# Score matmuls of a graph attention layer: two 64x128 array tiles or four 64x64 array tiles

## The chip, the cores and the metric

The kernel runs on one core of one Trainium2 chip. The metric is the device time of one execution in microseconds, the median of several runs. All data and all matmuls are in float32.

## The reference

For 128 graphs of 128 nodes with 768 features, a layer norm and a ReLU are followed by attention with 12 heads of 64 features. The adjacency matrix of each graph is both mask and bias of the scores. The result is added to the input.

```python
h = jnp.maximum(_layernorm(x, axis=-1), 0.0)
q = _split_heads(h @ Wq + bq)          # 12 heads of 64
k = _split_heads(h @ Wk + bk)
v = _split_heads(h @ Wv + bv)
scores = jnp.einsum('bhqd,bhkd->bhqk', q, k) / jnp.sqrt(HD)
scores = scores + beta * adj[:, None]
scores = jnp.where(adj[:, None] > 0, scores, -9e15)
probs = jax.nn.softmax(scores, axis=-1)
out = jnp.einsum('bhqk,bhkd->bhqd', probs, v)
x = x + out                            # heads side by side again
```

## The kernel before

Graphs are taken in 32 groups of four. The projections (Q, K and V) are computed by a scheme of 15 block products per slice of the output columns; each product is four matmuls of a full 128x128 weight tile with 256 moving columns:

```python
for i in range(2):
    for c in range(2):
        ...
        nc.tensor.matmul(p[:, i, :], lhs, rhs, start=(first and i == 0 and c == 0), stop=(c == 1),
                         skip_group_check=True)
```

The products are evicted and summed by ScalarE and VectorE (tiles pa, pb, pc and pd are the four banks that they go through). A tile `qk` holds, for two heads and two graphs, the queries in `t[:, 0]` and the keys in `t[:, 1]`, the 64 features of the first head on partitions 0 to 63 and those of the second on 64 to 127.

The scores of two heads (`oc`) and four graphs are eight matmuls. The keys are the stationary operand (64 rows, 128 columns), the queries the moving one (128 columns). Each head goes to its own bank of PSUM. The scores lie with the keys on the partitions:

```python
def scores(G, oc):
    u, j = oc // 3, oc % 3
    ...
    ps = [psum.tile([P, GRP, N], F32, tag="at", name=f"sc_{G}_{oc}_{i}") for i in range(2)]
    for g in range(GRP):
        t = qk[G, f"qk{u}", g // 2, j]
        at = slice((g % 2) * N, (g % 2 + 1) * N)
        for i in range(2):
            r = slice(i * HD, (i + 1) * HD)
            nc.tensor.matmul(ps[i][:, g, :], t[r, 1, at], t[r, 0, at], start=True, stop=True)
    for i in range(2):
        e = es[G, oc, i] = work.tile([P, GRP, N], F32, tag="e", name=f"e_{G}_{oc}_{i}")
        nc.vector.scalar_tensor_tensor(e, ps[i], SCORE_CAP * ISCALE, biasT[G], op0=ALU.min, op1=ALU.add)
        nc.scalar.activation(e, e, AF.Exp, scale=1.0 / ISCALE)
```

VectorE evicts them with the bias and the mask added, ScalarE takes the exponential in place. The product with V follows four block products later. Here the exponentials are the stationary operand, 64 queries at a time, so that the two halves go to the two halves of the array's columns; the moving operand is V with a column of ones beside it, 65 columns, which gives the sum of each softmax too:

```python
def attend(G, oc):
    o = work.tile([P, 2, 4, HD], F32, tag="o", name=f"o_{G}_{oc}", bufs=2)
    for r in range(2):
        pa = psum.tile([P, 4, VE], F32, tag="at", name=f"av_{G}_{oc}_{r}")
        for g in range(2):
            for i in range(2):
                h = 2 * oc + i
                for q in range(0, P, HD):
                    nc.tensor.matmul(pa[q:q + HD, 2 * g + i, :], es[G, oc, i][:, 2 * r + g, q:q + HD],
                                     vt[G, "v", r, h // 4][:, 4 * g + h % 4, :], start=True, stop=True)
        weigh(G, oc, r, pa, o[:, r])
    ...
```

`scores_half` and `attend_half` do the same for two graphs at a time and are used for three of the six head pairs of the last group. Scores and V products stand between the block products; of three score blocks in a slice the second and the third follow directly on a V block:

```python
def attention(G, u):
    todo = {}
    for i in range(3):
        todo.setdefault(1 + 4 * i, []).append(lambda oc=3 * u + i: scores(G, oc))
        todo.setdefault(5 + 4 * i, []).insert(0, lambda oc=3 * u + i: attend(G, oc))
    return todo
```

Of the kernel before, what the change touches and what calls it, by code (L numbers as in the profile page):

```python
# [106 lines left out]
def direct(ctx, tc, x, adj, wq, bq, wk, bk, wv, bv, beta, out, bad):  # L107
# [10 lines left out]
    nc = tc.nc  # L118
    B, N, D = x.shape
    HD = D // HEADS  # L120
# [224 lines left out]
    def scores(G, oc):  # L345
        u, j = oc // 3, oc % 3
        t = xo[G, oc] = work.tile([P, GRP, P], F32, tag="xo", name=f"xo_{G}_{oc}", bufs=3)
        nc.sync.dma_start(t, x[G * GRP:(G + 1) * GRP, :, oc * P:(oc + 1) * P].rearrange("g n d -> n g d"))
# [3 lines that stand above are left out]
            at = slice((g % 2) * N, (g % 2 + 1) * N)  # L352
            for i in range(2):
                r = slice(i * HD, (i + 1) * HD)
                nc.tensor.matmul(ps[i][:, g, :], t[r, 1, at], t[r, 0, at], start=True, stop=True)  # L355
        for i in range(2):
            e = es[G, oc, i] = work.tile([P, GRP, N], F32, tag="e", name=f"e_{G}_{oc}_{i}")
            nc.vector.scalar_tensor_tensor(e, ps[i], SCORE_CAP * ISCALE, biasT[G], op0=ALU.min, op1=ALU.add)  # L358
            nc.scalar.activation(e, e, AF.Exp, scale=1.0 / ISCALE)  # L359
# [27 lines left out]
    def scores_half(G, oc, r):  # L387

        u, j = oc // 3, oc % 3
        g0 = G * GRP + 2 * r  # L390
        t = xo[G, oc, r] = work.tile([P, 2, P], F32, tag="xo", name=f"xo_{G}_{oc}_{r}", bufs=3)
        nc.sync.dma_start(t, x[g0:g0 + 2, :, oc * P:(oc + 1) * P].rearrange("g n d -> n g d"))
        ps = [psum.tile([P, 2, N], F32, tag="at", name=f"sc_{G}_{oc}_{r}_{i}") for i in range(2)]
        t = qk[G, f"qk{u}", r, j]
        for g in range(2):
            for i in range(2):
                h = slice(i * HD, (i + 1) * HD)
                nc.tensor.matmul(ps[i][:, g, :], t[h, 1, g * N:(g + 1) * N], t[h, 0, g * N:(g + 1) * N],
                                 start=True, stop=True)
        e = es[G, oc, r] = work.tile([P, 2, 2, N], F32, tag="e", name=f"e_{G}_{oc}_{r}")  # L400
        for i in range(2):
            nc.vector.scalar_tensor_tensor(e[:, i], ps[i], SCORE_CAP * ISCALE, biasT[G][:, 2 * r:2 * r + 2, :],
                                           op0=ALU.min, op1=ALU.add)
            nc.scalar.activation(e[:, i], e[:, i], AF.Exp, scale=1.0 / ISCALE)
# [16 lines left out]
# [7 lines that stand above are left out]
# [72 lines left out]
    for G in range(NG):  # L500
# [27 lines left out]
        if G + 1 < NG:  # L528
            got = []
            at = 1 if G else 6  # L530
# [34 lines left out]
        for at, f, *args in (  # L565
            (0, scores, 0), (3, attend, 0), (3, scores, 1), (6, attend, 1), (6, scores, 2), (9, attend, 2),
            (9, scores_half, 5, 0), (10, scores_half, 4, 0), (11, attend_half, 5, 0), (12, scores_half, 3, 0),
            (12, attend_half, 4, 0), (13, scores_half, 3, 1), (13, attend_half, 3, 0), (14, scores_half, 5, 1),
            (14, attend_half, 3, 1), (14, scores_half, 4, 1), (14, attend_half, 5, 1), (14, attend_half, 4, 1),
        ):  # L570
            then(at, lambda f=f, args=args: f(G, *args))
# [143 lines left out]
```

## Time and profile before

| what | value |
|---|---|
| time, median of 3 runs | 3005.92 us (3005.69 to 3007.42) |
| span of the profiled run | 3006.0 us |
| granted TensorE clock | 0.998 |
| records of matmuls, and of weight loads | 20918 each |
| of these, scores on line 355 | 3024 |
| of these, V products on line 380 | 6048 |
| VectorE evictions of scores, 128x512 | 378, mean 684 ns |

In the lines of the profile, PE is TensorE's matmuls, PEld its weight loads, DVE VectorE, ACT ScalarE, POOL GpSimd. A name with an L is a line of the kernel. A pair such as 64*128 gives the rows and columns of the array that a matmul uses, and 64x128 behind it the partitions and columns of the operand read. Every float32 matmul of the program shows as two records of a weight load and two of a matmul. The recorded ends of matmuls are modelled and overlap, so the busy time of PE is not its streaming; the chain of work that ended last and the starts of single records say more.

### The profile page before, as it was taken

The numbers are of one execution on the slowest core, as the hardware profiler recorded it, in microseconds if no ns is written. First come the engines' busy times: TensorE is split into PE (matmuls) and PEld (weight loads), VectorE is DVE, ScalarE is ACT, GpSimd is POOL, SyncE is SP. The second block draws the span as 40 slices with busy tenths as digits, with TensorE's granted clock in tenths as the row PEclk, the third lists the DMA queues.
The fourth block names the chain that finished last, engine by engine and source line by source line (L and its number), as shares of the span: only waits on it lengthen the run. The fifth ranks groups of instructions, "written<-read, shape, count | busy, mean of one in ns | idle before, by whom it ended". The sixth has DMA issues, their size and how long they took to land.

```text
span 3006.0 us, 52526 instructions
## 1 busy us (share of the span) xinstructions
PE 2985.7 (99%) x20918; PEld 2579.4 (86%) x20918; DVE 1996.6 (66%) x5155; ACT 797.3 (27%) x1703; POOL 359.7 (12%) x307
## 2 busy tenths in 40 slices
PE   8999999999999999999999999999999999999998
PEld 7888888888888888888888888888888888888887
DVE  7867567676676665676656767567676676665665
ACT  2332322322223222222222232322322222222221
POOL 1111111111110111111111111111111110111110
PEclk9999999999999999999999999999999999999999
DMA  5212122121121211221212212122121122111211
GB/s 160 71 50 57 42 58 67 50 60 43 50 68 55 55 47 45 68 60 50 60 42 58 66 52 57 41 55 68 50 60 43 50 67 57 53 51 39 64 36 40
DMA packets 358505, 170.33 MB, mean 57 GB/s; under 512 B 84464, under 2 KB 358128, under 8 KB 358256
## 3 DMA queue, kind: packets, MB, share of 16 engines
q1 hardware_dynamic: 355392, 166.14, 20.1%
q8 instruction: 166, 2.72, 0.4%
q10 hardware_dynamic: 2864, 0.79, 0.1%
q14 instruction: 83, 0.68, 0.1%
HBM read 116.53 MB, written 50.33 MB: 56 GB/s over the span
## 4 chain that ended last, share of the span: by engine, by line
PE 98%; DVE 1%; DMA 0%; ACT 0%; issue 0%; SPq 0%; ACTq 0%; DVEq 0%
PE pc_qk L316 18%; PE pb_qk L316 15%; PE pa_qk L316 15%; PE pc_v L316 9%; PE pb_v L316 7%; PE pa_v L316 7%; PE pd_qk L316 7%; PE av L380 7%; PE sc L355 7%; PE pd_v L316 4%; PE plain L445 1%; DMA x<-in_x_dram 0%; ACT x L259 0%; DVE A L266 0%; DVE qk_T L199 0%; PE pm L228 0%
## 5 line engine op out<-in xcount | busy, mean ns | idle before, releaser
L384 POOL TENSOR_TENSOR xo<-xo,o 128x512 f32<-128x512 f32 x189 | 242.1, 1281 | 2330.5 <-DVE seen L370 2300.9
L359 ACT ACTIVATE e<-e 128x512 f32<-128x512 f32 x378 | 232.8, 630 | 691.4 <-DVE e L358 690.7
L259 ACT ACTIVATE x<-x,shift,rstd 128x192 f32<-128x192 f32 x512 | 228.0, 533 | 569.4 <-POOL shift L250 569.4
L316 PE MATMUL pb_qk<-S,qk_T 128*128 128x256 f32 x1512 | 370.3, 388 | 0.0
L337 ACT ACTIVATE qk<-pc_qk,bqk 128x256 f32<-128x256 f32 x378 | 160.4, 466 | 701.5 <-PE pc_qk L316 701.5
L358 DVE SCALAR_TENSOR_TENSOR e<-sc,biasT 128x512 f32<-128x512 f32 x378 | 242.8, 684 | 110.1 <-PE sc L355 110.1
L316 PEld LDWEIGHTS pb_qk<-S,qk_T 128*128 128x128 f32 x1512 | 277.3, 190 | 44.1
L341 DVE TENSOR_TENSOR qk<-qk,pb_qk 128x512 f32<-128x512 f32 x252 | 171.9, 682 | 146.5 <-PE pb_qk L316 125.7
L316 PE MATMUL pc_qk<-S,qk_B 128*128 128x256 f32 x1008 | 245.1, 386 | 2.3 <-ACT qk L337 2.3
L380 PEld LDWEIGHTS av<-v,e 128*64 128x64 f32 x6048 | 192.6, 138 | 62.9 <-issue 43.0
L316 PE MATMUL pa_qk<-S,qk_T 128*128 128x256 f32 x1008 | 244.8, 386 | 0.0
L316 PE MATMUL pc_qk<-S,qk_T 128*128 128x256 f32 x1008 | 238.2, 379 | 0.0
L266 DVE STREAM_TRANSPOSE A<-x 128x256 f32<-128x256 f32 x384 | 217.5, 611 | 7.4 <-ACT x L259 7.3
L355 PE MATMUL sc<-qk 64*128 64x128 f32 x3024 | 219.9, 285 | 0.0
L380 PE MATMUL av<-v,e 128*64 128x65 f32 x6048 | 218.8, 225 | 0.0
L316 PEld LDWEIGHTS pc_qk<-S,qk_B 128*128 128x128 f32 x1008 | 186.7, 190 | 32.7 <-ACT qk L337 2.7
L316 PEld LDWEIGHTS pc_qk<-S,qk_T 128*128 128x128 f32 x1008 | 191.8, 190 | 25.8
L316 PEld LDWEIGHTS pa_qk<-S,qk_T 128*128 128x128 f32 x1008 | 186.5, 190 | 30.2
L355 PEld LDWEIGHTS sc<-qk 64*128 64x128 f32 x3024 | 183.8, 188 | 29.6 <-issue 20.9
L316 PE MATMUL pb_v<-v_T,S 128*128 128x256 f32 x768 | 184.0, 383 | 0.0
L341 DVE TENSOR_TENSOR qk<-qk,pd_qk 128x512 f32<-128x512 f32 x126 | 86.7, 688 | 139.0 <-PE pd_qk L316 139.0
L272 DVE TENSOR_TENSOR S<-A,A 128x512 f32<-128x512 f32 x224 | 164.2, 747 | 1.0
(117 smaller groups left out, 4520.9 us busy)
## 6 DMA issues: line engine op xcount, KB each, us to landing
x<-in_x_dram SPq DMA_DIRECT2D x504, 96.0 KB, 2.4
xo<-in_x_dram SPq DMA_DIRECT2D x189, 256.0 KB, 2.9
out_dram<-xo SPq DMA_DIRECT2D x189, 256.0 KB, 2.2
adj<-in_adj_dram SPq DMA_DIRECT2D x128, 64.0 KB, 2.3
qk_T<-in_L_gnn_Wq_dram SPq DMA_DIRECT2D x10, 128.0 KB, 3.1
qk_T<-in_L_gnn_Wk_dram SPq DMA_DIRECT2D x10, 128.0 KB, 3.2
v_T<-in_L_gnn_Wv_dram SPq DMA_DIRECT2D x5, 256.0 KB, 6.0
qk_B<-in_L_gnn_Wq_dram SPq DMA_DIRECT2D x8, 128.0 KB, 3.3
```

Source lines behind the costliest of these rows:

```text
L259: nc.scalar.activation(t, t, AF.Relu, bias=shift[G, n], scale=rstd[G, n])
L266: last = nc.vector.transpose(t[:, :, g * N:(g + 1) * N].rearrange("p c (b i) -> p c b i", i=SQ), src)
L272: nc.vector.tensor_tensor(t, A[G, a], A[G, b], ALU.add if sign > 0 else ALU.subtract)
L316: nc.tensor.matmul(p[:, i, :], lhs, rhs, start=(first and i == 0 and c == 0), stop=(c == 1), skip_group_check=True)
L337: nc.scalar.activation(t[:, i, :], p[:, i, :], AF.Identity, bias=bqk[:, i, oc:oc + 1], scale=float(sign))
L341: added[G] = nc.vector.tensor_tensor(t, t, p, ALU.add if sign > 0 else ALU.subtract)
L355: nc.tensor.matmul(ps[i][:, g, :], t[r, 1, at], t[r, 0, at], start=True, stop=True)
L358: nc.vector.scalar_tensor_tensor(e, ps[i], SCORE_CAP * ISCALE, biasT[G], op0=ALU.min, op1=ALU.add)
L359: nc.scalar.activation(e, e, AF.Exp, scale=1.0 / ISCALE)
L380: nc.tensor.matmul(pa[q:q + HD, 2 * g + i, :], es[G, oc, i][:, 2 * r + g, q:q + HD], vt[G, "v", r, h // 4][:, 4 * g + h % 4, :], start=Tru ...
L384: nc.gpsimd.tensor_add(t, t, o.rearrange("p a (b j) d -> p (a b) (j d)", j=2))
L445: nc.tensor.matmul(p[:, i, :], b[:, c, i * P:(i + 1) * P], a[:, c, :], start=(k == 0 and i == 0 and c == 0), stop=(c == 1), skip_group_che ...
```

## The change

Each score matmul is split into two, of 64 keys each. The stationary operand is then 64 rows by 64 columns, and the two halves of the keys go to the two halves of the partitions of the same bank. With two heads this addresses four tiles of the array, 64x64 each, where before it was two, 64x128 each. The moving operand, the 128 queries, is unchanged and is streamed once for each half of the keys. The aim is to keep all four tiles at work, beside V matmuls which already use two column tiles.

```diff
             for i in range(2):
                 r = slice(i * HD, (i + 1) * HD)
-                nc.tensor.matmul(ps[i][:, g, :], t[r, 1, at], t[r, 0, at], start=True, stop=True)
+                for k in range(0, N, HD):
+                    nc.tensor.matmul(ps[i][k:k + HD, g, :], t[r, 1, at][:, k:k + HD], t[r, 0, at],
+                                     start=True, stop=True)
@@
                 h = slice(i * HD, (i + 1) * HD)
-                nc.tensor.matmul(ps[i][:, g, :], t[h, 1, g * N:(g + 1) * N], t[h, 0, g * N:(g + 1) * N],
-                                 start=True, stop=True)
+                for k in range(0, N, HD):
+                    nc.tensor.matmul(ps[i][k:k + HD, g, :], t[h, 1, g * N + k:g * N + k + HD],
+                                     t[h, 0, g * N:(g + 1) * N], start=True, stop=True)
```

The second part of the diff is in `scores_half`.

## The prediction

> **What bounds the kernel now.** I read the page's first two parts, then the chain that ended last, then the waits, and last the matmuls of one short stretch.
>
> ```profile
> PE 2985.7 (99%) x20918; PEld 2579.4 (86%) x20918; DVE 1996.6 (66%) x5155; ACT 797.3 (27%) x1703; POOL 359.7 (12%) x307
> ...
> PE 98%; DVE 1%; DMA 0%; ACT 0%; issue 0%; SPq 0%; ACTq 0%; DVEq 0%
> PE pc_qk L316 18%; PE pb_qk L316 15%; PE pa_qk L316 15%; PE pc_v L316 9%; PE pb_v L316 7%; PE pa_v L316 7%; PE pd_qk L316 7%; PE av L380 7%; PE sc L355 7%; PE pd_v L316 4%; PE plain L445 1%; DMA x<-in_x_dram 0%; ACT x L259 0%; DVE A L266 0%; DVE qk_T L199 0%; PE pm L228 0%
> ```
>
> TensorE is 98% of the chain, so the time is what the matmul stream takes from end to end. The score matmuls (tile sc) are 7% of it, some 210 us of 3006; the V matmuls (av) are another 7%. In the list of waits TensorE waits for VectorE, ScalarE and the transfers about 15 us in all, nearly all at the start and the end, and VectorE is busy 66%: no other engine is close. The granted clock is 0.998.
>
> A piece of the chain from the middle of the run, columns start us, length us, what:
>
> ```profile
> 1017.65 1.73 PE pa_qk L316 x8
> 1019.38 1.08 PE av L380 x32
> 1020.46 1.09 PE sc L355 x16
> 1021.55 1.93 PE pc_qk L316 x8
> 1023.48 1.73 PE pb_qk L316 x8
> ```
>
> Eight records of a product take 1.73 us, 216 ns each, but 1.93 us behind scores: the way out of a score block costs 0.20 us. With the 1.09 us of the block itself, **a score block costs the stream 1.29 us**. There are 189 such blocks (3024 records of 16 each) and six half-sized ones in the last group. Each fp32 matmul of the program is two records, a pass each: 1536 score matmuls, 3072 records.
>
> The same stretch, asked for sc and for av (minimum/median/maximum ns):
>
> ```profile
> L355 PEld LDWEIGHTS sc<-qk x16: 183/188/189, 1020.4 to 1021.2; 64*128 64x128 f32 x16
> L355 PE MATMUL sc<-qk x16: 272/272/373, 1020.4 to 1021.3; 64*128 64x128 f32 x16
> ...
> L380 PEld LDWEIGHTS av<-v,e x32: 133/138/140, 1019.3 to 1020.2; 128*64 128x64 f32 x32
> L380 PE MATMUL av<-v,e x32: 219/222/271, 1019.3 to 1020.2; 128*64 128x65 f32 x32
> ```
>
> The first matmuls of a score block last 373 ns and the others 272: the first ones stand 101 ns waiting for their own weights, 128 columns. The first V matmuls wait only 271 - 222 = 49 ns, for 64 columns. Record by record, the score matmuls start in pairs, 6 ns apart, one in each half of the array's rows, and the pairs follow each other every 112 ns: eight rounds. The V matmuls also start in pairs, one in each half of the columns, every 59 ns. Ahead of both blocks, and behind the scores, lies a pause: from where the last matmul should have ended streaming to the next weight load some 95 ns pass (last product start 1018.998[...], first V load 1019.306). So the 1.29 us are about 95 pause + 101 weights + 8 x 112 rounds + 95 pause + 105 weights of the product behind (its first matmul takes 484 where the others take 379), which is 1292 ns.
>
> **What the Trainium skill says.** "TensorEngine Tiling (Array Packing)", Key Properties: changing the tiling mode, unlike changing the tile, drains the engine, and tiles can load and multiply side by side. The trace agrees with both: the 95 ns pause stands at each switch, and the pairs overlap. "TensorE: Matmul & The Clock Gate", LDWEIGHTS: a load costs by its columns, not its rows; the 101 ns for 128 columns and 49 ns for 64 agree. The same page, Part 3, gives about 4 ns per tile of stagger and speedups for 16 small tiles; the trace shows 6 ns, with two tiles only. "PSUM — Partial Sum Buffer", bank collisions: column tiles may write one bank together, row tiles may not. Here the row halves write different banks (ps[0] and ps[1]) before and after. No run so far shows four tiles together.
>
> **The change part by part.** It replaces each 64x128 score matmul by two of 64x64. Score matmuls go from 1536 to 3072, records from 3072 to 6144, and loads likewise, each of 64 columns in place of 128. The moving data stays 128 queries, so a matmul streams as long as before (112 ns a round). A full block becomes 32 records; with four tiles at work at once that is again 32 / 4 = **eight rounds of 112 ns**, no fewer. The array was already fully covered by two 64x128 tiles; a finer cut gives no throughput. What changes is at the edges:
>
> - The exposed first weight load falls from 101 to 49 ns: -52 ns a block, on the path.
> - The third and fourth tile start behind the second by 6 ns each: +12 ns a block, on the path.
> - The pauses at the switches stay: the mode ahead is still a different one (whole array, or 128 rows by 64 columns), and so is the product's behind. 0.
> - The product's first weights behind the block have 128 columns as before: 0.
>
> Sum: -40 ns a block, times 189, is -7.6 us; the six half blocks add -0.2. That makes **3005.9 - 7.8 = 2998 us**.
>
> Comparing the order of the built instructions: on TensorE the sequence of products, scores and V blocks is the same; ScalarE and GpSimd have no change of order; VectorE has its 5232 instructions in a somewhat different order (for instance in the middle groups a sum of activations S<-A,A moves ahead of a score eviction). As the evicted scores are needed four products (7 us) later, and one such sum takes 0.75 us, I count this as 0, with a few us of doubt at the start, where the waits of TensorE lie.
>
> **The rivals.**
>
> 1. Four tiles do not run at once. If only two of the four advance together, a block takes 16 rounds: + 8 x 112 = 0.90 us a block, x 189 = +169 us, 3175 us. For it: this kernel has never shown four tiles, and each matmul's two passes stand together in the program, so the engine must look past six records to reach the fourth tile. Against it: two row tiles and two column tiles both overlap fully now, from their first round on, with the same kind of double passes. I give it one chance in fifteen.
>
> 2. The supply of instructions becomes the bound. A score block would use up 32 loads and 32 matmuls in 0.90 us, a pair each 28 ns. The V block already keeps a pair each 59 / 2 = 29 ns for 32 pairs. But 126 score blocks follow directly on V blocks (as in the stretch above), where today 48 pairs pass in 1.08 + 1.09 = 2.17 us, 45 ns a pair, and afterwards 64 must pass in about the same time, 33 ns a pair. Nothing in the profile shows a run of 64 pairs at that pace. If 45 ns were the sustained limit, 64 x 45 = 2.88 us, +0.71 x 126 = +90 us, 3095 us. One chance in fifteen, with smaller versions of it possible.
>
> 3. The switch between two column-tiled modes (128x64 to 64x64) costs no drain. Then 126 blocks save the pause of 95 ns and hide the remaining 49 ns of weights besides: -0.144 x 126 = -18 us, 2980 us. For it: the columns are cut alike in both. Against it: the skill speaks of the mode as a whole, and every change of shape in this trace has its pause. One chance in eight.
>
> 4. VectorE becomes the bound through its new order. It idles a third of the time, so at most a few us.
>
> **Range and chances.** The centre is the sum, 2998. The lower end leaves room for the cheap switch, 2976. The upper end takes a mild shortage of instructions (some 0.2 us in each of the 126 blocks, +25 us) or a few more ns a round, 3032; the two full bad cases lie above it. Faster by over 2% would need 60 us out of blocks whose streaming cannot shrink: 0.32 us of each 1.29, more than all that the edges offer short of losing both pauses; 1%. Slower by over 2% are rivals 1 and 2 in full: 12%.
>
> **What would show it.** In the profile after: score matmuls about 6050 on their main line, still near 272 ns, and their loads near 138 in place of 188; a block's share of the chain 1.05 us in place of 1.09 (the first step right), with the product behind it still 1.93 (the pauses stayed). Records in fours, 6 ns apart, every 112 ns show the eight rounds; fours that fall into two pairs 112 ns apart are rival 1; rounds that begin at 112 ns and stretch later in a block, most of all behind V blocks, are rival 2. A score block behind V well below 1 us with no pause ahead is rival 3. The prediction is wrong if a round costs more than 112 ns with four tiles for a reason that the pairs do not show, such as loads or moving reads of the four tiles getting in each other's way: each 10 ns a round is 8 x 189 x 10 ns = 15 us.

## The result and the profile after

The changed kernel takes 2995.95 us (median of 6 runs), the kernel before in the same sessions 3006.78 us: a ratio of 0.9964, 95% interval 0.9951 to 0.9977. That is 10.8 us less, well outside the spread of either kernel (2.4 us); the prediction had 7.8 us less, 2998 us, and a range of 2976 to 3032.

The page after, its first part and the chain that ended last:

```profile
PE 2974.5 (99%) x23990; PEld 2555.1 (85%) x23990; DVE 1996.6 (67%) x5155; ACT 797.8 (27%) x1703; POOL 373.7 (12%) x307
...
PE 98%; DVE 1%; DMA 0%; ACT 0%; issue 0%; SPq 0%; ACTq 0%; DVEq 0%
```

TensorE is still 98% of the chain. It has 3072 more records of matmuls and as many more loads, and yet ends 11 us earlier. The piece of the chain of the changed kernel that answers to the one of before (start us, length us, what):

```profile
1016.15 1.08 PE av L382 x32
1017.23 1.03 PE sc L356 x32
1018.26 1.93 PE pc_qk L316 x8
```

The score block has fallen from 1.09 to 1.03 us; the V block ahead and the product behind are unchanged to the hundredth. And the score records of that stretch (minimum/median/maximum ns):

```profile
L356 PEld LDWEIGHTS sc<-qk x32: 129/133/133, 1017.2 to 1017.9; 64*64 64x64 f32 x32
L356 PE MATMUL sc<-qk x32: 269/269/320, 1017.2 to 1018.0; 64*64 64x128 f32 x32
```

The first matmuls now wait 320 - 269 = 51 ns for their weights, before it was 101. And the common duration is 269 ns in place of 272: a small difference, but one that comes again in the rounds (a round is the time from one record of a tile to the next of the same tile). From record to record, the starts of the first tile's matmuls in this block are 160, 269, 378, 487, 597, 706, 815 ns after the first one, **109.2 ns a round**; the same list before reads 214, 325, 438, 549, 660, 772, 884, that is 111.7 ns a round. In each round the four tiles start 6 to 7 ns apart, the last one 20 ns behind the first.

Counted from the end of the last product matmul ahead to the end of the first one behind, less the 216 ns of one product record, a score block alone costs 1289 ns before and 1231 ns after (the median of 63 blocks each). The 58 ns are made up of 51 for the first weights, plus 20 for the eight rounds (2.5 each), less 13 for the later start of the last tile. Over 189 blocks that is 11.0 us, and the profiled spans differ by 3006.0 - 2995.2 = 10.8 us. So the score blocks hold all of it, and the changed order of VectorE's instructions holds nothing that could be seen: the waits of TensorE's matmuls for other engines are the same list, with the same numbers to within 0.2 us.

Two rounds give an estimate of what streaming alone takes, if a column takes the same time in both. A product record with 256 moving columns follows the one before it by 215.8 ns, a changed score record with 128 columns by 109.2: 106.6 ns for 128 columns more, or 0.83 ns a column, and some 2.5 ns for each record besides. By this estimate the last product record ahead of a block streams for 213 ns, and of the 308 ns from its start to the first load behind it 95 are the pause.

### The profile page after: what moved, and what is told of

It is laid out like the page before. It is cut to its first block, busy times and chain, and to the rows that moved or that the text cites. A ratio compares the mean times of both kernels' runs of the same rounds, so it can differ in the third digit from the quotient of the medians.

```text
span 2995.2 us, 58670 instructions
## 1 busy us (share of the span) xinstructions
PE 2974.5 (99%) x23990; PEld 2555.1 (85%) x23990; DVE 1996.6 (67%) x5155; ACT 797.8 (27%) x1703; POOL 373.7 (12%) x307
## 4 chain that ended last, share of the span: by engine, by line
PE 98%; DVE 1%; DMA 0%; ACT 0%; issue 0%; SPq 0%; ACTq 0%; DVEq 0%
PE pc_qk L316 18%; PE pb_qk L316 15%; PE pa_qk L316 15%; PE pc_v L316 9%; PE pb_v L316 7%; PE pa_v L316 7%; PE pd_qk L316 7%; PE av L382 7%; PE sc L356 6%; PE pd_v L316 4%; PE plain L448 1%; DMA x<-in_x_dram 0%; ACT x L259 0%; DVE A L266 0%; DVE qk_T L199 0%; PE pm L228 0%
## 5 line engine op out<-in xcount | busy, mean ns | idle before, releaser
L386 POOL TENSOR_TENSOR xo<-xo,o 128x512 f32<-128x512 f32 x189 | 256.0, 1354 | 2305.8 <-DVE seen L372 2254.2
L356 PE MATMUL sc<-qk 64*64 64x128 f32 x6048 | 208.7, 275 | 0.0
L356 PEld LDWEIGHTS sc<-qk 64*64 64x64 f32 x6048 | 162.9, 132 | 29.6 <-issue 20.9
```

The lines of the kernel that those rows point to most:

```text
L356: nc.tensor.matmul(ps[i][k:k + HD, g, :], t[r, 1, at][:, k:k + HD], t[r, 0, at], start=True, stop=True)
L386: nc.gpsimd.tensor_add(t, t, o.rearrange("p a (b j) d -> p (a b) (j d)", j=2))
```

## The experiments

The first two ask why a round became shorter, the next two how far TensorE looks ahead (on which the four tiles at once depend), then what the pause at a switch is, and the last uses the answer.

### Moving queries halved, two tiles

```diff
-                nc.tensor.matmul(ps[i][:, g, :], t[r, 1, at], t[r, 0, at], start=True, stop=True)
+                for k in range(0, N, HD):
+                    nc.tensor.matmul(ps[i][:, g, k:k + HD], t[r, 1, at], t[r, 0, at][:, k:k + HD],
+                                     start=True, stop=True)
```

> Scores as before (two 64x128 tiles), but the moving queries in two halves of 64, so 16 rounds of half the streaming in each block. Theory 1, the round before (112 ns) is set by the load of 128 weight columns[...]: 16 rounds of 112 ns, some +0.84 us a block, times 189, about 3165 us. Theory 2, the round is the streaming plus some 5 ns that belong to the mode with two tiles: 16 rounds of 58 ns, a block stays near 1.29 us, 3000 to 3012 us. The first matmul waits 101 ns for its weights in both.

Measured: 3171.51 us, a ratio to the kernel before of 1.0546 (1.0528 to 1.0563). A piece of its chain:

```profile
1008.30 1.08 PE av L382 x32
1009.39 1.98 PE sc L356 x32
...
L356 PEld LDWEIGHTS sc<-qk x32: 182/188/188, 1009.3 to 1011.0; 64*128 64x128 f32 x32
L356 PE MATMUL sc<-qk x32: 272/272/320, 1009.3 to 1011.1; 64*128 64x64 f32 x32
```

With half the streaming in each matmul and the same 128 weight columns, a tile still takes 111.7 ns a record, as much as before, and the block takes 1.98 us in place of 1.09. Theory 1 holds: **with 128 weight columns a tile takes 111.7 ns a round, whether it streams 128 columns or 64.** The round of the kernel before was set by its weight loads and not by the streaming; that the two lie within a few ns of each other (111.7 and 109.2) hid it.

### Moving queries halved, four tiles

```diff
-                for k in range(0, N, HD):
-                    nc.tensor.matmul(ps[i][k:k + HD, g, :], t[r, 1, at][:, k:k + HD], t[r, 0, at],
-                                     start=True, stop=True)
+                for s in range(0, N, HD):
+                    for k in range(0, N, HD):
+                        nc.tensor.matmul(ps[i][k:k + HD, g, s:s + HD], t[r, 1, at][:, k:k + HD],
+                                         t[r, 0, at][:, s:s + HD], start=True, stop=True)
```

> The changed kernel (four 64x64 tiles) with the moving queries in two halves of 64: 64 records a block. Theory 1, a load of 64 columns fits into a round of 58 ns as it does in the V blocks: 16 rounds of 58 ns = 0.93 us against 0.87 us, +0.06 us a block, about 3006 us. Theory 2, streaming plus 2.4 ns: 16 rounds of 56 ns, about 2999 us. Rival, the supply of instructions ends at about one pair of load and matmul each 28 ns, the fastest seen so far: 64 pairs take 1.8 us, +0.9 us a block, about 3170 us, with rounds that stretch late in the block.

Measured: 3017.17 us, ratio to before 1.0032 (1.0021 to 1.0044).

```profile
L357 PEld LDWEIGHTS sc<-qk x64: 129/135/135, 1023.2 to 1024.1; 64*64 64x64 f32 x64
L357 PE MATMUL sc<-qk x64: 218/218/267, 1023.2 to 1024.2; 64*64 64x64 f32 x64
...
1023.26 1.14 PE sc L357 x62
```

(The chain follows 62 of the block's 64 records.) The later rounds are 58.3 ns, which is nearer to theory 1: by the estimate above, 64 streamed columns would go round in 56. The V blocks point the same way. They load 64 weight columns and stream 65, and their rounds are 58.5 ns; were streaming the limit, the column more would show as 0.8 ns and not as 0.2. So the 58 ns are read as the load of 64 columns.

The block is 0.11 us longer than the changed kernel's, where 0.06 was expected. The third and fourth tile, those of the second head, start 27 and 33 ns after the first one instead of 13 and 20. Their fifth records then last 252 ns instead of 218, because their weights were not loaded ahead, and from there on these two tiles are 35 ns late. Why was not tried on its own, but it fits the full waiting line that the next experiments show: here a tile gets four records in a turn, and the fifth ones of the second head stand behind the eighth of the first tile. The run with two tiles above shows the same: the second head's fifth record lasts 313 ns instead of 272.

What falls is the rival of a short supply: 64 loads and 64 matmuls start within 0.99 us, a pair each 15 ns, where the V blocks had one each 29.

### Tile by tile

```diff
-        for g in range(GRP):
-            ...
-            for i in range(2):
-                r = slice(i * HD, (i + 1) * HD)
-                for k in range(0, N, HD):
-                    nc.tensor.matmul(...)
+        for i in range(2):
+            r = slice(i * HD, (i + 1) * HD)
+            for k in range(0, N, HD):
+                for g in range(GRP):
+                    ...
+                    nc.tensor.matmul(...)
```

> The changed kernel with the order of the 16 score matmuls changed: all four of one tile first, then the next tile. Nothing else. If TensorE looks far ahead in its queue (past 24 records of matmuls and as many loads), all four tiles still run together and the time stays at 2996 us. If it looks ahead only over some records, tiles run one or two at a time: two at a time gives 16 rounds, +0.87 us a block, 3160 us; one at a time 32 rounds, +2.6 us a block, 3490 us.

Measured: 3267.99 us, ratio 1.0867 (1.0849 to 1.0885), between the two bad cases. A piece of its chain:

```profile
1001.01 2.50 PE sc L356 x32
1003.51 1.92 PE pc_qk L316 x8
```

The same 16 matmuls in another order take 2.50 us in place of 1.03. Read record by record, the first tile runs alone at 0, 160, 269 and 378 ns; its fifth record starts at 487, and 6 ns later, at 493, the second tile starts its first. At that moment three records of the first tile, the sixth to the eighth, are still waiting. The same is seen at each change of tile.

### Two graphs for each tile

```diff
-        for g in range(GRP):
-            t = qk[G, f"qk{u}", g // 2, j]
-            at = slice((g % 2) * N, (g % 2 + 1) * N)
+        for p in range(0, GRP, 2):
+            t = qk[G, f"qk{u}", p // 2, j]
             for i in range(2):
                 r = slice(i * HD, (i + 1) * HD)
                 for k in range(0, N, HD):
-                    nc.tensor.matmul(...)
+                    for g in (p, p + 1):
+                        at = slice((g % 2) * N, (g % 2 + 1) * N)
+                        nc.tensor.matmul(...)
```

> The changed kernel with the order of the score matmuls changed less far than in tile_by_tile: two graphs (four records) of one tile, then two of the next, round the four tiles, twice. Model 1, each tile has a waiting line of its own that takes three records besides the running one, and the engine hands out records in order until one meets a full line: all four tiles get work at once, a block keeps its 0.87 us of rounds, 2996 us. Model 2, the engine looks past no more than three waiting records in all, wherever they wait: the third tile starts only when the first two are nearly through, some two tiles at a time, +0.6 us a block, about 3110 us.

Measured: 3008.35 us, ratio to before 1.0004 (0.9995 to 1.0012): 12 us more than the changed kernel, 100 less than model 2 had.

```profile
1021.47 1.10 PE sc L357 x32
1022.57 1.92 PE pc_qk L316 x8
```

All four tiles start at once, at 0, 13, 26 and 40 ns, with 3 x 3 = 9 records of the first three tiles ahead of the fourth tile's first in the program and still waiting: model 2, three waiting records in all, falls. **Each tile has a line of its own that takes the running record and three more.** Where the program has more than that for one tile, the engine stops handing out until the line moves. This shows in the middle of the block: the first tile's fifth record starts on time at 487 ns; the fifth of the second, third and fourth are handed out only then, when nothing waits in their lines any more, and three matmuls last 312 to 313 ns in place of 269 because their weights were not loaded ahead. These 44 ns and the later start of the fourth tile (40 ns behind the first one, 20 in the changed kernel) are the 64 ns that a block has become longer, 12 us over 189 blocks. My expectation of 2996 us was wrong in this. Model 1 as stated would have given it, had I followed the line into the second half of the block.

In the changed kernel a tile gets two records in turn, and nothing of the kind shows: behind the first round every record lasts 269 ns.

### V matmuls in 64 rows by 64 columns

```diff
-                        nc.tensor.matmul(pa[q:q + HD, 2 * g + i, :], es[G, oc, i][:, 2 * r + g, q:q + HD],
-                                         vt[G, "v", r, h // 4][:, 4 * g + h % 4, :], start=True, stop=True)
+                        w = slice(r * HD, (r + 1) * HD)
+                        nc.tensor.matmul(pa[q:q + HD, 2 * g + i, :], es[G, oc, i][w, 2 * r + g, q:q + HD],
+                                         vt[G, "v", r, h // 4][w, 4 * g + h % 4, :], start=True, stop=True)
```

> The changed kernel with the V matmuls on 64 rows and 64 columns too (they leave out half of the keys: keys 0 to 63 for the first two graphs, 64 to 127 for the others), so that V and scores use one tiling mode. Theory, the pause belongs to the change of mode: between V and scores it falls from 95 ns to near 0 and the first score weights are loaded beside the last V matmuls, -0.14 us in 126 blocks, -18 us. Rival, the pause belongs to the change of operands or the wait for the semaphore: it stays at 95 ns. Apart from this the V block itself may shorten from 0.94 us towards 0.5 us if its two row halves run together (up to another -85 us); it keeps its length if they don't because 16 records lie between them.

Measured: 9795.9 us. This time says nothing of the question: with half of the keys left out some queries have no neighbour left, their softmax sums fall to the floor, and the kernel's guard then computes everything a second time on a general path. The first part of its trace, ahead of that second pass, gave the expectation for the next run, which has the guard's limit raised and still leaves out half of the keys:

```diff
-SUM_CAP = 1e15
+SUM_CAP = 1e32
```

> v_in_64_row_tiles with the limit on the softmax sums raised, so that the second pass through the general path, which rows without any key had set off, does not run: V matmuls on 64 rows and 64 columns, half of the keys left out. By the first part of the trace of v_in_64_row_tiles (a V block with scores behind it costs 1.98 us in place of 2.31, a V block alone 1.10 in place of 1.28): 126 x 0.33 + 63 x 0.18 = 53 us less, 2943 us. The rival that the pause belongs to the operands or semaphores would leave the 95 ns between V and scores in place.

Measured: 2943.71 us, ratio to before 0.9789 (0.9773 to 0.9805). Its records of TensorE in order of time, between a V block and the scores behind it (start us, length us):

```profile
1008.01 0.80 PE L383 MATMUL av<-v,e 64*64 64x65 f32 x26
1008.60 0.33 PE L356 MATMUL sc<-qk 64*64 64x128 f32 x2
1008.65 0.28 PE L383 MATMUL av<-v,e 64*64 64x65 f32 x4
1008.76 0.27 PE L356 MATMUL sc<-qk 64*64 64x128 f32 x1
1008.77 0.22 PE L383 MATMUL av<-v,e 64*64 64x65 f32 x1
1008.77 0.27 PE L356 MATMUL sc<-qk 64*64 64x128 f32 x1
1008.77 0.22 PE L383 MATMUL av<-v,e 64*64 64x65 f32 x1
1008.82 1.04 PE L356 MATMUL sc<-qk 64*64 64x128 f32 x28
```

The first scores start at 1008.60, while six V records are still to start. Their weight loads wait for VectorE's semaphore as before, and their operands change as before; only the change of mode is gone, and with it the pause. It is not that the scores merely find idle rows: the later ones run on the rows of the last V matmuls and start some 50 ns behind them (1008.77 and 1008.82). **The pause is the change of mode.** A V block with scores behind it costs 1980 ns in place of 2314; part of the 334 ns is that the V block itself runs partly in four tiles (alone it costs 1105 in place of 1280). If it saves the same ahead of scores, about 160 ns are the switch; 95 of pause and some 50 of weights now loaded beside the last V matmuls make up most of them. As half of the contraction is left out, this is a measurement and no version to use.

### Blocks joined

```diff
-        todo = {}
-        for i in range(3):
-            todo.setdefault(1 + 4 * i, []).append(lambda oc=3 * u + i: scores(G, oc))
-            todo.setdefault(5 + 4 * i, []).insert(0, lambda oc=3 * u + i: attend(G, oc))
-        return todo
+        a, b, c = 3 * u, 3 * u + 1, 3 * u + 2
+        return {
+            2: [lambda: scores(G, a), lambda: scores(G, b)],
+            6: [lambda: attend(G, a), lambda: attend(G, b)],
+            9: [lambda: scores(G, c)],
+            13: [lambda: attend(G, c)],
+        }
```

> The changed kernel with fewer changes of mode: of the three score blocks of a slice the first two stand together, and so do their two V blocks; the third of each stands alone (8 changes of mode in place of 10). By the durations of the changed kernel a half of a group costs 1.23 + 0.87 (scores), 1.28 + 0.94 (V), 1.23, 1.28 = 6.83 us in place of 1.23 + 2 x 2.31 + 1.28 = 7.14 us: -0.3 us, times 63, about 2977 us. Rival: two score blocks take all four score banks of PSUM and two V blocks too, and TensorE waits for their evictions by VectorE, some tenths of a us each time: the gain is lost, 2990 to 3020 us, with waits of TensorE for VectorE or ScalarE in the list of waits.

Measured: 2979.01 us, ratio to before 0.9907 (0.989 to 0.9923). Nothing is left out; this is the fastest full version. From its chain:

```profile
1004.75 1.91 PE sc L356 x64
1006.65 1.92 PE pc_qk L316 x8
...
1013.76 2.02 PE av L382 x64
1015.77 1.92 PE pb_qk L316 x8
...
1021.15 1.03 PE sc L356 x32
```

Two score blocks together take 1.91 us, the second adding 0.87 and no pause, and two V blocks 2.02. So with one kind of matmul behind the same kind there is no pause here either, in a kernel that computes everything. The rival's waits did not come. Of TensorE's list of waits, the only line that the kernels before and after don't have is

```profile
PE pa_qk L316 <- DVE qk L341: 0.7, 1, 0.7
```

once, 0.7 us. The gain over the changed kernel, some 17 us, is larger than that of the change itself. By the costs of the blocks, a half of a group (one slice of queries and keys, three head pairs) takes 6.83 us in place of 7.14, as expected; over 63 halves that would be 19 us, of which 17 showed. It comes from two changes of mode fewer in each half. The blocks also stand at other places among the products now (2, 6, 9 and 13); those that stand alone cost the same as before, 1231 and 1280 ns.

## Why the prediction was right, point by point

- **The bound.** TensorE's stream carries the span before and after, and the whole difference lies in the score blocks (11.0 us by their costs, 10.8 by the spans).
- **Eight rounds, four tiles at once.** Right: records come in fours, 6 to 7 ns apart, from the first round on.
- **The first weights, -52 ns.** Measured -51.
- **The stagger, +12 ns.** Measured +13.
- **The pauses and the product behind, 0.** Measured 0: the way from the last product to the first load is 307 ns before and 308 after, from the last V start to the first score load 148 ns, and from the last score end to the first product end 413 ns, in both kernels.
- **The length of a round, 112 ns and unchanged.** This term was mis-sized. It is 109.2 ns after, -20 ns a block, -3.8 us in all, and this accounts for the measured 10.8 us where 7.8 were forecast. I had taken the 112 ns for the streaming. Halving the streaming with the load kept left the round at 111.7 ns: it was the load of 128 columns. Halving the load therefore gives the round back to the streaming, which for 128 columns comes to 109 ns. So the statement that a matmul "streams as long as before" held, and the conclusion that the round stays did not.
- **VectorE's new order, 0.** No wait of TensorE's matmuls shows it.
- **Rival 1** did not come, but was closer than I thought: it is a matter of order. With the tiles one after another it would have cost 272 us against the changed kernel's order. My ground against it, that two tiles already overlapped in spite of double passes, was sound for the order of this change alone.
- **Rival 2** falls in the trace after: the 64 pairs of a V block and the scores behind it pass in 1.08 + 1.03 = 2.11 us, 33 ns a pair. The pace of a pair each 15 ns in another run shows how far off that limit was.
- **Rival 3** falls in the trace after: the pause between 128x64 and 64x64 is unchanged. Columns cut alike are not enough; in the experiment with one mode, where the rows are cut alike too, the pause is gone.

On what the Trainium skill says of draining at a change of mode ("TensorEngine Tiling (Array Packing)", Key Properties): the runs agree, and put a size to it, about 95 ns of pause by the estimate above, with the exposed first weights behind it, 49 to 51 ns for 64 columns and 101 to 105 for 128.

## What to carry to other kernels

Here, cutting matmuls into smaller tiles of the array gained no throughput, as the larger tiles already covered it: the streaming stayed at eight rounds. It shortens the weight load, which counts at the edges of a block and wherever a load is as long as the streaming beside it. Each change of tiling mode cost a pause and a load that nothing hid, so put work of one mode together before cutting anything finer. Deal matmuls out round the tiles in small turns: the same 16 matmuls took 1.03 us dealt round and 2.50 us tile by tile.

## What the runs showed of the hardware that I had not expected

- A tile's round has two floors: its streaming, 109.2 ns for 128 columns, and its weight load, 111.7 ns for 128 columns and 58.3 ns for 64. In the four combinations measured, the longer one sets it.
- Each tile has a waiting line of its own, of three records beside the running one, and a full line holds up the others (2.50 us tile by tile, 1.10 us two graphs at a time, 1.03 us dealt round).
- With one mode on both sides, the first matmuls of a later block started while six records of the earlier block, which stand ahead of them in the program, had not started yet.
- Four tiles took a load and a matmul each 15 ns, over 64 pairs; the one delay in it, 35 ns in two of the tiles, fits a full line.
